# A layer of test-time training with a routed feed-forward block: GpSimd sums F for the bias, the inverse's join moves one place, and K and Q of 23 steps come from seven products of halves

## The chip, the core and the metric

The kernel runs on one NeuronCore of a Trainium2 chip. The core has a matrix engine (TensorE; PE in the profile, with its weight loads as PEld), a vector engine (VectorE, DVE), a scalar engine (ScalarE, ACT), a general one (GpSimd, POOL) and a queue that mostly issues transfers (SyncE, SP). Each engine works through its own instructions in order and waits for the others by semaphores. The metric is the time of one execution on the device in microseconds (us), the median of several runs.

## What is computed

The input is x, 2 sequences of 4096 tokens with 512 features. The first half of the block is a linear model that is trained while it reads: for every token, in order,

```python
pred = W @ k + b
g = 2.0 / d_h * (pred - v)
W = W - LR * jnp.outer(g, k)
b = b - LR * g
out = W @ q + b
```

with k, v, q = theta_K x, theta_V x, theta_Q x. Then x + out goes through a layer norm. The second half is a shared two-layer network plus the two best of eight experts for each token (a routed mixture), added to its input and normed again. Everything is float32.

## The kernel before

**Tiles and steps.** The tokens of both sequences are cut into 32 chunks of 128 (NCH = 32, and B = 2 sequences are handled side by side). Within a chunk the 128 sequential updates are solved at once: with A = 1 + K K^T of the chunk, the updates F are the solution of a triangular system, which the kernel gets by inverting a 128x128 triangular matrix. So the loop over chunks, not over tokens, is sequential: step c needs the W and b that step c-1 left.

**The parts of one round.** In round c four generators run beside each other, and their matmuls are woven together by `interleave`: it always advances the part whose yielded work is the smallest share of its total. The totals are numbers written out by hand.

- `step(c)`, total 49.0: R = -V + K W + b (`pr`, then the add L437 on VectorE with the bias tile `brep[s]`), the first part of the output (`po`, Q times W), the last part of the inverse (`join`), F (`pe`, copied by ScalarE to R, scaled by -BETA, L481), the output's correction with AQ (L485), the update of W (`pw` L491, added by VectorE L492), and the update of the bias: `pb` L497 multiplies F by a matrix of ones, which puts the sum of F over its 128 tokens in each of 128 partitions, and L498 adds that to `brep[s]`. GpSimd adds `brep[s]` to x ahead of the output (L439).
- `prep(c + 1)`, total 13.5: the next chunk's K and Q (`pkq` L327), their products `pa`, the block's diagonal parts sent through DRAM to L, and, for the chunks in `TURNED` (1 to 23), a copy of K transposed with the help of DRAM (`exchange`, later `turn_blocks` on VectorE). GpSimd masks A (L353) and copies the start value X (L361).
- `invert(c)`, total 95.0: the 32x32 diagonal blocks' inverses on VectorE (L372), then through DRAM to D and DT.
- `shared(c - 1)`, total 13.5: layer norm, the shared network and the router of the chunk before. GpSimd adds a bias (L627) and scatters the tokens' places with indirect transfers (L585).

From round 24 on the routed experts come in as a fifth part: `routed` gathers tokens (L809) and weights (L815) with indirect transfers on GpSimd's queue, each three tiles ahead. After that, `collect` fetches and sums the results.

**K and Q.** For each of theta_K and theta_Q, `prep` makes four blocks of 128 output features. Each block is 4 matmuls of 128x128 weights with the 256 tokens of both sequences as the moving operand; a float32 matmul stands in the profile as two MATMUL rows. So a chunk has 2 x 16 matmuls, 64 rows, of 256 columns. ScalarE copies the results to the tile KQ in 8 pieces (L334). The accumulators have the tag `pp`, of which there are two buffers, shared with `pa` and with the join's `pn` and `pz`.

**The join.** `join` is a generator of four pieces: one matmul pair with a copy by ScalarE (`pn`, N), then three times a matmul pair and an add by VectorE (`pz`, Z). `next(levels)` runs one. In the chunks 1 to 23 they come after the second sequence's R, in the middle and at the end of the first `po`, and in the middle of the second `po`; the last Z is Y, the left operand of `pe`.

**Orders.** On PE and VectorE instructions run in the order in which the program issues them (`manual_schedule`). For the other queues a scheduler sets the order, by when it reckons an instruction's inputs to be ready; each queue is then served strictly in that order.

Of the kernel before, what the change touches and what calls it, by code (L numbers as in the profile page):

```python
# [33 lines left out]

# [6 lines left out]
F32 = mybir.dt.float32  # L41
# [3 lines left out]
ALU = mybir.AluOpType  # L45
AX = mybir.AxisListType

P = 128
# [8 lines left out]
KQ_PACE, X_PACE, C_PACE = 1.0, 0.7, 10.0  # L57
PREP, INVERT = 13.5, 95.0
SKIP = 1 << 20

TURNED = range(1, 24)
PSUM = bass.MemoryType.PSUM
# [41 lines left out]
def postln_block(ctx: ExitStack, tc: tile.TileContext, x, xT, thK, thV, thQ, w0, b0, masks, blk,  # L104
# [211 lines left out]

    prepared, turned = {}, {}

    def prep(c):
        xt = xT_t[c]  # L320
        KQ = kqp.tile([P, DC, B, 2, P], F32, tag="kq", name=f"kq_{c}")
        for j, th in enumerate((thK_sb, thQ_sb)):
            for ec in range(0, DC, 2):
                ps = ps_p.tile([P, 2, B, P], F32, tag="pp", name=f"pkq_{c}_{j}_{ec}")
                for i in range(2):
                    for dc in range(DC):
                        nc.tensor.matmul(  # L327
                            ps[:, i].rearrange("p s t -> p (s t)"),
                            th[:, dc, (ec + i) * P:(ec + i + 1) * P],
                            xt[:, dc].rearrange("p s t -> p (s t)"),  # L330
                            start=(dc == 0), stop=(dc == DC - 1))
                    yield KQ_PACE
                for i in range(2):
                    nc.scalar.copy(KQ[:, ec + i, :, j, :], ps[:, i])  # L334
# [18 lines left out]
        nc.gpsimd.tensor_tensor(M, A1, mask[:, 0:1, :].broadcast_to([P, B, P]), ALU.mult)  # L353
# [7 lines left out]
        nc.gpsimd.tensor_copy(X, unit_sb)  # L361
# [55 lines left out]
    def step(c):  # L417
# [6 lines left out]
        for s in range(B):  # L424
            ps = ps_s.tile([P, D], F32, tag="ps", name=f"pr_{c}_{s}")
            for dc in range(DC):
                nc.tensor.matmul(ps, xt[:, dc, s, :], nthV_sb[:, dc, :],  # L427
                                 start=(dc == 0), stop=False)
                if dc % 2 == 1:
                    yield 2.0  # L430
            for ec in range(DC):
                nc.tensor.matmul(ps, KQ[:, ec, s, 0, :], W[s][:, ec, :],  # L432
                                 start=False, stop=(ec == DC - 1))
                if ec == 1:
                    yield 2.0
# [3 lines left out]
            nc.gpsimd.tensor_tensor(xc[:, s, :], xc[:, s, :], brep[s], ALU.add)  # L439
            if s == B - 1:  # L440
                next(levels)
            yield 2.5
        for s in range(B):

            ps = ps_s.tile([P, D], F32, tag="ps", name=f"po_{c}_{s}")
            for ec in range(DC):
                nc.tensor.matmul(ps, KQ[:, ec, s, 1, :], W[s][:, ec, :],  # L447
                                 start=(ec == 0), stop=False)
                if ec == 1:
                    if s == 0:  # L450
                        next(levels)
                    elif c in TURNED:
                        Y = next(levels)
                    yield 2.0
            O.append(ps)
            if s == 0:
                next(levels)
            yield 2.0
            if s == 0:

                if c not in TURNED:
                    Y = next(levels)
# [21 lines left out]
        for s in range(B):  # L484
# [3 lines left out]
            if c < NCH - 1:  # L488
                for ec in range(DC):
                    ps = ps_s.tile([P, D], F32, tag="ps", name=f"pw_{c}_{s}_{ec}")  # L490
                    nc.tensor.matmul(ps, K[s][:, ec, :], F[s], start=True, stop=True)  # L491
                    nc.vector.tensor_tensor(W[s][:, ec, :], ps, W[s][:, ec, :], ALU.add)  # L492
                    if s > 0 and ec == 1:
                        next(norm[0])
                    yield 1.0
                ps = ps_s.tile([P, D], F32, tag="ps", name=f"pb_{c}_{s}")
                nc.tensor.matmul(ps, ones, F[s], start=True, stop=True)  # L497
                nc.vector.tensor_tensor(brep[s], ps, brep[s], ALU.add)  # L498
# [222 lines left out]
    def plan(gr):  # L721
# [63 lines left out]
        sl = tmp("sl", [P, n])  # L785
# [275 lines left out]
```

## Time and profile before

| | |
|---|---|
| median of 3 runs | 2716.18 us (2708.08 to 2716.97) |
| the profiled execution | 2700.66 us, of which the span from first to last instruction is 2698.9 us |
| granted TensorE clock, mean | 0.986 |
| VectorE busy | 1272.1 us (47%), 4016 instructions |
| ScalarE busy | 759.8 us (28%), 1516 instructions |
| GpSimd busy | 763.3 us (28%), 767 instructions |
| K and Q matmuls (L327) | 2048 rows, busy 242.5 + 243.8 us |
| bias sums (`pb`, L497) | 124 rows, busy 63.8 us |
| bias adds (L498) | 62, mean 686 ns |

A group of the profile gives line, engine, operation, output and inputs by the program's names, the shapes, the number of instructions, their busy time and mean, and how long the engine was idle just before them and for what. Two cautions: a matmul's row lasts longer than the distance to the next one, since matmuls overlap in the array, so a PE that is "busy" need not be full; and the cost of a matmul in a stream is the distance between starts, not its row's length. A timeline's row merges equal neighbours: start, duration from the first start to the last end, and "x8" for eight of them.

The first step begins at 38.3 us and the steps 1 to 22 take 60.46 us each, from first `pr` to first `pr`. The rounds 24 to 27 with the routed tiles take 170, 166, 167 and 148 us, the rounds 28 to 30 between 67 and 75 us, and what follows the start of the last step 356 us.

### The profile page before, as it was taken

What the parts mean: (1) busy time and instruction counts of PE and PEld (TensorE: products, weight loads), DVE (VectorE), ACT (ScalarE), POOL (GpSimd) and SP (SyncE); (2) the same over time, 40 slices, a digit from 0 to 9 for tenths busy, and PEclk for the clock granted to TensorE, in tenths of its full rate; (3) what the DMA queues carried; (4) which work ended last, traced back from release to release, by engine and by line L of the source; (5) the groups of instructions that cost most, each with busy time, mean ns of one, the idle gap of its engine ahead of it and who ended that gap; (6) DMA issues with size and microseconds to landing.
All of it is one profiled execution on the core that took longest, in us unless ns stands there. A gap on an engine that the chain in (4) does not pass through costs nothing. (4 is left out here: it accounts for less than half of the span.)

```text
span 2698.9 us, 31214 instructions
## 1 busy us (share of the span) xinstructions
PE 2588.6 (96%) x10381; PEld 1654.4 (61%) x10381; DVE 1272.1 (47%) x4016; ACT 759.8 (28%) x1516; POOL 763.3 (28%) x767
## 2 busy tenths in 40 slices
PE   8999999999999999999999999999999989879887
PEld 5665666666656666666655666767666655446564
DVE  2555554455555554555556223232232466644245
ACT  1222222222222222222222232322223133434336
POOL 0111111111111111112123333343343334455555
PEclk9999999999999999999999999999999999989898
DMA  5122222222222222222233343353433345676677
GB/s 181 52 64 73 64 57 67 71 57 56 57 73 64 64 57 70 67 57 57 59 97 117 125 91 106 119 152 99 123 102 92 117 127 166 183 244 214 232 244 235
DMA packets 257712, 293.48 MB, mean 109 GB/s; under 512 B 158332, under 2 KB 171868, under 8 KB 253968
## 3 DMA queue, kind: packets, MB, share of 16 engines
q1 hardware_dynamic: 199536, 163.62, 20.1%
q0 software_dynamic: 49584, 111.61, 14.5%
q10 hardware_dynamic: 8432, 16.25, 1.9%
q8 instruction: 83, 1.36, 0.2%
q14 instruction: 77, 0.63, 0.1%
HBM read 345.43 MB, written 100.69 MB: 165 GB/s over the span
## 5 line engine op out<-in xcount | busy, mean ns | idle before, releaser
L372 DVE SCALAR_TENSOR_TENSOR X<-L,X 128x31 f32<-128x31 f32 (+22 forms) x1472 | 327.3, 269 | 26.3 <-DMA L<-dL 9.2
L833 PEld LDWEIGHTS phe<-gT,wb 128*128 128x128 f32 x2208 | 269.0, 193 | 63.7 <-issue 57.0
L847 DVE TENSOR_TENSOR o<-pye,wb 128x512 f32<-128x512 f32 x138 | 95.4, 691 | 427.3 <-PE pye L844 402.4
L844 PE MATMUL pye<-wb,he 128*128 128x512 f32 x552 | 273.4, 619 | 16.5 <-ACT he L837 15.5
L833 PE MATMUL phe<-gT,wb 128*128 128x128 f32 x2208 | 271.7, 277 | 8.1 <-DMA wb<-wcat_in,widx 6.8
L585 POOL DMA_INDIRECT gt<-code,ri x124 | 124.5, 1004 | 542.8 <-DVE ri L582 512.7
L491 PE MATMUL pw<-R,K 128*128 128x512 f32 x496 | 234.7, 604 | 15.7 <-DVE x L486 13.4
L327 PE MATMUL pkq<-xT,thK 128*128 128x256 f32 x1024 | 242.5, 381 | 7.4 <-DMA thK<-thK_in 7.4
L327 PE MATMUL pkq<-xT,thQ 128*128 128x256 f32 x1024 | 243.8, 382 | 2.7 <-DVE Z L411 2.7
L447 PE MATMUL po<-W,kq 128*128 128x512 f32 x512 | 245.9, 604 | 0.0
L815 POOL DMA_INDIRECT wb<-wcat_in,widx x138 | 145.3, 1053 | 332.1 <-DVE o L847 166.8
L327 PEld LDWEIGHTS pkq<-xT,thK 128*128 128x128 f32 x1024 | 195.1, 191 | 71.4 <-issue 49.0
L427 PE MATMUL pr<-thV,xT 128*128 128x512 f32 x512 | 238.0, 596 | 0.0
L432 PE MATMUL pr<-W,kq 128*128 128x512 f32 x512 | 231.9, 592 | 0.0
L837 ACT ACTIVATE he<-phe,wb 128x128 f32<-128x128 f32 x276 | 87.2, 364 | 422.0 <-PE phe L833 420.8
L327 PEld LDWEIGHTS pkq<-xT,thQ 128*128 128x128 f32 x1024 | 186.2, 191 | 28.2 <-issue 4.8
L492 DVE TENSOR_TENSOR W<-pw,W 128x512 f32<-128x512 f32 x248 | 168.3, 689 | 64.2 <-PE pw L491 63.7
L334 ACT COPY kq<-pkq 128x256 f32<-128x256 f32 x256 | 83.0, 375 | 407.7 <-PE pkq L327 407.7
L809 POOL DMA_INDIRECT g<-gy,gidx x138 | 139.3, 1009 | 134.2 <-PE pg L824 104.9
L844 PEld LDWEIGHTS pye<-wb,he 128*128 128x128 f32 x552 | 99.9, 192 | 119.8 <-issue 80.6
L491 PEld LDWEIGHTS pw<-R,K 128*128 128x128 f32 x496 | 89.7, 192 | 131.2 <-issue 76.3
L427 PEld LDWEIGHTS pr<-thV,xT 128*128 128x128 f32 x512 | 94.3, 190 | 99.5 <-issue 79.4
(207 smaller groups left out, 3366.6 us busy)
## 6 DMA issues: line engine op xcount, KB each, us to landing
ge<-o SPq DMA_DIRECT2D x138, 256.0 KB, 2.0
xT<-xT_in SPq DMA_DIRECT2D x32, 512.0 KB, 3.6
x<-x_in SPq DMA_DIRECT2D x32, 512.0 KB, 3.5
L<-dL SPq DMA_DIRECT2D x128, 128.0 KB, 2.9
gy<-x SPq DMA_DIRECT2D x31, 512.0 KB, 2.7
gb<-x SPq DMA_DIRECT2D x31, 512.0 KB, 2.7
acc<-gb POOLq DMA_DIRECT2D x31, 512.0 KB, 6.5
y_out<-acc ACTq DMA_DIRECT2D x31, 512.0 KB, 5.0
```

The lines of the kernel that those rows point to most:

```text
L327: nc.tensor.matmul(ps[:, i].rearrange("p s t -> p (s t)"), th[:, dc, (ec + i) * P:(ec + i + 1) * P], xt[:, dc].rearrange("p s t -> p (s t) ...
L372: nc.vector.scalar_tensor_tensor(X[:, h, j + 1:], L[:, j + 1:, j], X[:, h, j:j + 1], X[:, h, j + 1:], ALU.mult, ALU.add)
L427: nc.tensor.matmul(ps, xt[:, dc, s, :], nthV_sb[:, dc, :], start=(dc == 0), stop=False)
L432: nc.tensor.matmul(ps, KQ[:, ec, s, 0, :], W[s][:, ec, :], start=False, stop=(ec == DC - 1))
L447: nc.tensor.matmul(ps, KQ[:, ec, s, 1, :], W[s][:, ec, :], start=(ec == 0), stop=False)
L491: nc.tensor.matmul(ps, K[s][:, ec, :], F[s], start=True, stop=True)
L492: nc.vector.tensor_tensor(W[s][:, ec, :], ps, W[s][:, ec, :], ALU.add)
L585: nc.gpsimd.indirect_dma_start(out=gr.tables[s * K + k], out_offset=bass.IndirectOffsetOnAxis(ap=ri[:, s, k:k + 1], axis=0), in_=code[:, j ...
L809: nc.gpsimd.indirect_dma_start(out=g_t[k], out_offset=None, in_=gr.y, in_offset=bass.IndirectOffsetOnAxis(ap=gr.gidx[:, k:k + 1], axis=0), ...
L815: nc.gpsimd.indirect_dma_start(out=wbuf[k % NW], out_offset=None, in_=wcat, in_offset=bass.IndirectOffsetOnAxis(ap=gr.widx[:, k:k + 1], ax ...
L833: nc.tensor.matmul(ps[:, hc, :], w[:, dc * HF + hc * P:dc * HF + (hc + 1) * P], t[:, dc, :], start=(dc == 0), stop=(dc == DC - 1))
L844: nc.tensor.matmul(ps, h[:, hc, :], w[:, O2 + hc * D:O2 + (hc + 1) * D], start=(hc == 0), stop=(hc == HC - 1))
```

## The change

Three edits. First, the sum of F over the tokens is made on GpSimd (`partition_all_reduce` into a new tile `ar`, one buffer), and GpSimd adds it to the bias; the matmul with ones, its accumulator, the add on VectorE and the tile of ones go. Second, the four pieces of the join come one place later, and at the same places in all chunks: middle and end of the first `po`, middle and end of the second. Third, in the chunks 2 to 24 K and Q come from `seven`, Strassen's scheme: theta is split in halves of rows and columns, x in halves of the input features (low, high) and by sequence. The four blocks of a 2x2 by 2x2 product then take seven products of halves, of sums and differences of blocks, where the plain form takes eight. K and Q are done together (index j). The five combinations of theta are made once, at the start, in the buffers of the experts' weights, which are free until round 23; the five combinations of x are made in each round by GpSimd. Five of the seven products are copied out by ScalarE, GpSimd makes two sums of three of these, and VectorE adds each of the last four blocks from a product in PSUM and a saved tile.

The totals of `step` in `interleave` become 44.0 and 46.5. In `plan` the tile `sl` shares the buffer of `has`.

```diff
-    ones = const.tile([P, P], F32, tag="ones", name="ones")
-    nc.gpsimd.memset(ones, 1.0)
...
+    comb = [[] for _ in range(5)]
+    for i, th in enumerate((thK_sb, thQ_sb)):
+        a11, a21, a12, a22 = (th[:, d:d + DC // 2, e:e + D // 2] for d in (0, DC // 2)
+                              for e in (0, D // 2))
+        t = wbuf[i][:, 0:5 * D].rearrange("p (n d e) -> p n d e", n=5, d=DC // 2)
+        for n, (p, q, op) in enumerate(((a11, a22, ALU.add), (a21, a22, ALU.add),
+                                        (a11, a12, ALU.add), (a21, a11, ALU.subtract),
+                                        (a12, a22, ALU.subtract))):
+            nc.gpsimd.tensor_tensor(t[:, n], p, q, op)
+            comb[n].append(t[:, n])
...
+    def seven(c, KQ):
...
+        for n, (p, q, op) in enumerate(((b11, b22, ALU.add), (b12, b22, ALU.subtract),
+                                        (b21, b11, ALU.subtract), (b11, b12, ALU.add),
+                                        (b21, b22, ALU.add))):
+            nc.gpsimd.tensor_tensor(sums[:, n], p, q, op)
+        saved, made = {}, {}
+
+        def product(name, half, x_half):
+            ps = ps_p.tile([P, DC // 2, 2, P], F32, tag="pp", name=f"pkq_{c}_{name}")
+            made[name] = ps
+            for i in range(DC // 2):
+                for j in range(2):
+                    for dc in range(DC // 2):
+                        nc.tensor.matmul(ps[:, i, j, :], half[j][:, dc, i * P:(i + 1) * P],
+                                         x_half[:, dc, :],
+                                         start=(dc == 0), stop=(dc == DC // 2 - 1))
+
+        def save(name, tag):
+            m = cp.tile([P, DC // 2, 2, P], F32, tag=tag, name=f"m{name}_{c}")
+            nc.scalar.copy(m, made[name])
+            saved[name] = m
+
+        def block(h, s, name, other):
+            nc.vector.tensor_tensor(KQ[:, h, s], made[name], saved[other], ALU.add)
...
+        def total(name, tag, p, q, r, op):
+
+            d = cp.tile([P, DC // 2, 2, P], F32, tag=tag, name=f"m{name}_{c}")
+            nc.gpsimd.tensor_tensor(d, saved[p], saved[q], op)
+            nc.gpsimd.tensor_tensor(d, d, saved[r], ALU.add)
+            saved[name] = d
+
+        pace = 8 * KQ_PACE / 7
+        product(5, comb[2], b22)
+        save(5, "z00")
+        yield pace
+        product(4, half_of(high, 1), sums[:, 2])
+        save(4, "z01")
+        yield pace
+        product(1, comb[0], sums[:, 0])
+        save(1, "z10")
+        total("451", "z01", 4, 5, 1, ALU.subtract)
+        yield pace
+        product(2, comb[1], b11)
+        save(2, "z11")
+        block(high, 0, 2, 4)
+        yield pace
+        product(3, half_of(low, 0), sums[:, 1])
+        save(3, "z00")
+        block(low, 1, 3, 5)
+        total("123", "z10", 1, 2, 3, ALU.subtract)
+        yield pace
+        product(7, comb[4], sums[:, 4])
+        block(low, 0, 7, "451")
+        yield pace
+        product(6, comb[3], sums[:, 3])
+        yield pace
+        block(high, 1, 6, "123")
+        yield 0.3
...
             nc.gpsimd.tensor_tensor(xc[:, s, :], xc[:, s, :], brep[s], ALU.add)
-            if s == B - 1:
-                next(levels)
             yield 2.5
...
                 if ec == 1:
-                    if s == 0:
-                        next(levels)
-                    elif c in TURNED:
-                        Y = next(levels)
+                    next(levels)
                     yield 2.0
             O.append(ps)
-            if s == 0:
-                next(levels)
+            Y = next(levels)
             yield 2.0
...
-                ps = ps_s.tile([P, D], F32, tag="ps", name=f"pb_{c}_{s}")
-                nc.tensor.matmul(ps, ones, F[s], start=True, stop=True)
-                nc.vector.tensor_tensor(brep[s], ps, brep[s], ALU.add)
-                yield 1.0
+
+                ar = stepp.tile([P, D], F32, tag="ar", name=f"ar_{c}_{s}", bufs=1)
+                nc.gpsimd.partition_all_reduce(ar, F[s], P, bass_isa.ReduceOp.add)
+                nc.gpsimd.tensor_tensor(brep[s], ar, brep[s], ALU.add)
...
-        parts = [(49.0, step(c))]
+        parts = [(44.0 if c in TURNED else 46.5, step(c))]
```

More of the change, by code (lines that the diff above doesn't have):

```diff
@@ L35 @@
 import concourse.bass as bass
+import concourse.bass_isa as bass_isa
 import concourse.tile as tile
@@ L59 @@
 SKIP = 1 << 20
+SEVEN = range(2, 25)
 TURNED = range(1, 24)
@@ L317, in postln_block, with half_of @@
     prepared, turned = {}, {}
+    def seven(c, KQ):
+        xt = xT_t[c]
+        low, high = slice(0, DC // 2), slice(DC // 2, DC)
+        b11, b12, b21, b22 = (xt[:, h, s, :] for h in (low, high) for s in range(B))
+        sums = wbuf[2][:, (c % 2) * 5 * D // 2:(c % 2 + 1) * 5 * D // 2].rearrange(
+            "p (n d t) -> p n d t", d=DC // 2, t=P)
+        for n, (p, q, op) in enumerate(((b11, b22, ALU.add), (b12, b22, ALU.subtract),
[18 more added lines that the diff above has]
+            nc.vector.tensor_tensor(KQ[:, h, s], made[name], saved[other], ALU.add)
+        def half_of(h, k):
+            return [t[:, h, k * D // 2:(k + 1) * D // 2] for t in (thK_sb, thQ_sb)]
+        def total(name, tag, p, q, r, op):
[30 more added lines that the diff above has]
+        yield 0.3
@@ L321, in prep @@
         KQ = kqp.tile([P, DC, B, 2, P], F32, tag="kq", name=f"kq_{c}")
[L322 to L334, printed above, removed]
+        if c in SEVEN:
+            yield from seven(c, KQ)
+        else:
+            for j, th in enumerate((thK_sb, thQ_sb)):
+                for ec in range(0, DC, 2):
+                    ps = ps_p.tile([P, 2, B, P], F32, tag="pp", name=f"pkq_{c}_{j}_{ec}")
+                    for i in range(2):
+                        for dc in range(DC):
+                            nc.tensor.matmul(
+                                ps[:, i].rearrange("p s t -> p (s t)"),
+                                th[:, dc, (ec + i) * P:(ec + i + 1) * P],
+                                xt[:, dc].rearrange("p s t -> p (s t)"),
+                                start=(dc == 0), stop=(dc == DC - 1))
+                        yield KQ_PACE
+                    for i in range(2):
+                        nc.scalar.copy(KQ[:, ec + i, :, j, :], ps[:, i])
         A1 = prepp.tile([P, B, P], F32, tag="A1", name=f"A1_{c}", bufs=1)
@@ L449, in step @@
                 if ec == 1:
-                    if s == 0:
-                        next(levels)
-                    elif c in TURNED:
-                        Y = next(levels)
+                    next(levels)
                     yield 2.0
             O.append(ps)
-            if s == 0:
-                next(levels)
+            Y = next(levels)
             yield 2.0
             if s == 0:
-                if c not in TURNED:
-                    Y = next(levels)
                 if c < NCH - 1:
@@ L784, in plan @@
         nc.vector.tensor_tensor(adj, adj, step[:, None, :].broadcast_to(full), ALU.mult)
-        sl = tmp("sl", [P, n])
+        sl = tmp("has", [P, n], "sl")
         nc.vector.tensor_reduce(sl, adj, AX.X, ALU.add)
```

## The prediction

> **What bounds the kernel now.** I read the page's busy shares and slices first, then one steady round in a table of stretches, then the timelines of PE and of GpSimd inside it. The page:
>
> ```profile
> span 2698.9 us, 31214 instructions
> ...
> PE 2588.6 (96%) x10381; PEld 1654.4 (61%) x10381; DVE 1272.1 (47%) x4016; ACT 759.8 (28%) x1516; POOL 763.3 (28%) x767
> ...
> PE   8999999999999999999999999999999989879887
> ...
> POOL 0111111111111111112123333343343334455555
> ```
>
> PE is at 9 from the second slice to the 32nd; GpSimd at 1 up to the 18th. "Busy" can mislead on PE, so I take distances between starts. PE's timeline of round 24 has all three widths side by side:
>
> ```profile
> 1511.71 1.88 PE L844 MATMUL pye<-wb,he 128*128 128x512 f32 x4
> 1513.42 1.89 PE L327 MATMUL pkq<-xT,thK 128*128 128x256 f32 x8
> 1515.15 1.95 PE L833 MATMUL phe<-gT,wb 128*128 128x128 f32 x16
> 1516.93 0.60 PE L824 MATMUL pg<-ident,g 128*128 128x128 f32 x4
> ```
>
> Start to start: 4 rows of 512 columns in 1.71 us (0.427 each), 8 of 256 in 1.73 (0.215), 16 of 128 in 1.78 (0.111). Columns are all that is paid for. With 0.427, 0.213 and 0.107 us a row, one round of steps 1 to 22 adds up to: `pkq` 64 x 0.213 = 13.65, `pr` 32 x 0.427 = 13.65, `po` and `pw` 6.83 each, `pa`, `ph` and `py` 3.4 to 3.5 each, `pe`, AQ, `pb` and the join 1.71 each, transposes and router 1.6: 59.7 us. The round lasts 60.46. So PE is full to 0.75 us, and what leaves PE leaves the time, as long as nothing else becomes late.
>
> **Removed from PE.** `pb` is 4 rows of 512 a round: 4 x 0.427 = 1.71 us, in 31 rounds 52.9 us. Two adds on VectorE (L498, 0.69 us) go with it. K and Q: seven products of 8 matmuls, 56 matmuls, 112 rows of 128 columns: 112 x 0.107 = 11.95 us against 13.65, so 1.71 us a round and 39.3 us in 23 rounds. Together **92.2 us** at most, 3.42 us of a round of 60.46.
>
> Here a rule speaks against the change. The Trainium skill, "TensorE: Matmul & The Clock Gate", section "Back-to-back issue gap", gives for streams of weight load and matmul about 81 ns at 128 columns and 131 ns at 512: a column costs 2.5 times more in narrow matmuls. Halfway between (some 106 ns at 256, my estimate), a narrow column would cost 1.5 times that of `pkq`: 112 rows would take 18.3 us, and the 23 rounds would lose 107 us. The row of `phe`, with new weights for each of its 16 rows, shows 0.111 against 0.215; even that 0.111 leaves 112 x 0.111 = 12.4. The trace decides: 12.0 to 12.4 us.
>
> **Other engines.** ScalarE: 8 copies of 0.375 us (L334) become 5 of 128x512, by the row of L606 0.61: 3.0 us both times. VectorE: four new adds from PSUM at 0.69 (the row of L492), two fewer: +1.4 us on 36.8 a round of 57; it stays under the cover of PE. If an add is late, the next product waits, as `pp` has two buffers; I put 0.3 us a round on this. The once-made combinations of theta are 10 GpSimd adds of 1.27 us (the row of L439), 12.7 us at the start, where GpSimd stands idle to 23.09 us; they are needed after 87 us: nothing. No transfer is added. That of K through DRAM (`exchange`) now waits for the last block instead of the middle of the round, some 18 us later on SP's queue; its reader is the next round's `turn_blocks` over 40 us on, and its landing took 2.7 and 3.0 us: nothing. In round 23 the first weight gathers wait for the last products that read those buffers; a few us of GpSimd, covered.
>
> **The join one place later.** I weave the parts by hand with the new totals. Behind the last `pz` PE has one `py` (1.7 us) before `pe`, and Z takes 0.28 + 0.42 plus signals: covered. Between first and second `pz` stands half a `po` (1.7 us): covered. In step 0 `pn` waited 3.76 us for D; half a `po` now goes first: about 1 us gained, not counted. The removed last place before the second half of `po` costs nothing.
>
> **GpSimd is what is new on the path.** Its steady round now:
>
> ```profile
> 1035.33 1.03 POOL L585 DMA_INDIRECT gt<-code,ri  x1 [23.60 <-DVE ri L582]
> ...
> 1039.23 0.98 POOL L585 DMA_INDIRECT gt<-code,ri  x1 [0.30 <-issue]
> 1046.33 0.72 POOL L353 TENSOR_TENSOR A<-A,mask 128x256 f32<-128x256 f32 x1 [6.12 <-DMA dL<-A]
> 1050.06 1.27 POOL L439 TENSOR_TENSOR x<-x,brep 128x512 f32<-128x512 f32 x1 [3.01 <-DVE brep L498]
> 1055.43 1.26 POOL L439 TENSOR_TENSOR x<-x,brep 128x512 f32<-128x512 f32 x1 [4.11 <-DVE brep L498]
> 1062.10 2.49 POOL L627 TENSOR_TENSOR x<-x,b 128x512 f32<-128x512 f32 x2 [5.41 <-PE pt L604]
> 1072.06 0.24 POOL L361 COPY X<-unit 128x64 f32<-128x64 f32 x1 [7.46 <-DMA dX<-X]
> ```
>
> Ten us of work in 60. Added: 5 sums of 128x256 at 0.73 (L353) = 3.6; 4 adds of 128x512 at 1.27 for the two totals = 5.1; 2 bias adds = 2.5; and two all-reduces of length *a* each. The sum with gaps between scatters is 22 + 2a. A second unknown is *r*, the price of a change between all-reduce and ordinary add, of which each round has four.
>
> Bounds. *a*: no row shows it. From below, one pass of 128x512 on this engine is 1.27 us, and it must be read and written while 128 partitions are summed: two passes, 2.5 us. From above, the Trainium skill, "GPSIMD Engine Reference", section "Cross-partition — where GPSIMD wins", has 247.7 us for a reduction over partitions at 128x2048, which makes 62 us at 512 columns (estimate). The ends are far apart; nearest is the row of 1.27 us, and I take 5 to 6 passes, **7 us** (an estimate from that row). *r*: GpSimd's rows of different kinds follow each other with no gap (a gather of 1.00 us at 1517.81, the copy X at 1518.81), so 0 from below; the same page, section "Instruction dispatch", has about 6 us for the first call after a kernel's code has been loaded. I take the rows' value, near **0**, and keep 6.
>
> The deadline. In the woven order F of the first sequence is ready at about 42 us of a round of 57, behind it the scatters end near 46. R of the second sequence (L437), which needs the second bias, comes at 25 us of the next round, and VectorE is strictly in order: behind R stands the add that frees the accumulator which the sixth product in line needs, so PE stalls from about 27. That leaves 38 us, less 8 for what else is in line (bias adds 2.5, A 0.7, the two of L439 2.5, L627 2.5): PE feels nothing while **2a + 3r < 30**, and GpSimd has room while 2a + 4r < 35. My values give 14. If r is 6, they give 32 and 38, just over.
>
> In rounds 24 to 27 token gathers stand behind the all-reduces. They are issued three tiles, some 17 us, ahead, and land in 8.5: a block of 8 us is nearly covered, and 8 such blocks cost about 8 us. The fetches of rounds 28 to 30 (6 blocks) lose about 6.
>
> **Sum.** 92.2 - 7 (0.3 us in 23 rounds) - 8 - 6 = 71 us, 2.6%. The profiled execution would go from 2700.66 to 2630 us; the median lies 15.5 above that execution and goes to **2645 us**. With nothing lost it is 2624; with double the losses 2666.
>
> **Rivals.**
> - GpSimd late (slower): each round waits for the bias. It decides above 2a + 3r = 30, and turns the sign at about 34, when the overrun eats 3.4 us a round; r = 6 with a = 9 is 36, or 42 of GpSimd's own time against 35: a round of about 64, +3.5 us in 23 rounds = +80, and in the routed rounds 14 blocks of 22 us, each some 5 past its cover, +70, less 12 for `pb`: about 2850. For it speaks the page's 6 us; against it GpSimd's idle 50 us and gapless rows. Chance 0.33.
> - All-reduce at the price of the page's reduction, 62 us: a GpSimd round of 146 us, +86 in 31 rounds: about 5400. Against it: GpSimd's adds here are within 2 to 4 times a VectorE add, far from 50 times; 0.04.
> - Narrow matmuls as the rule has them: +107 - 53 + 21 = +75, about 2790. Against it stands the row of `phe`; 0.02.
> - Gain and overrun cancel (2a + 3r near 33): 2708 to 2724; 0.05.
> - The products don't shorten K and Q because PE waits for sums or accumulators, but `pb`'s gain stays: 2716 - 53 + 14 = 2677. Against: each product has about 5 us till the buffer is needed again. 0.08, faster.
>
> The likeliest, 0.48, is 2645 with a range of 2620 to 2670. A measurement can tell about 0.3% (8 us) from no change. Faster 0.56, same 0.05, slower 0.39. The range runs from 2612 to 2850: it holds the forecast, the smaller gain, the tie and most of the late cases.
>
> **What would show it.** Right: rounds of 57.0 to 57.5 us from `pr` to `pr`, 112 `pkq` rows of 128x128 at 0.107 apart, R of both sequences waiting for PE, not for GpSimd, and all-reduces under 10 us. Wrong: L437 waiting for GpSimd's bias with PE idle behind it, gaps after each all-reduce on GpSimd, or `pg` waiting for its gather.

## The result, and where the time went

The changed kernel takes **2872.05 us** in the median (2846.91 to 2884.71, 4 runs) beside 2716.57 us before (4 runs): 1.057 times the time, 95% interval 1.049 to 1.064. The forecast of 2645 us was wrong in sign, and the time lies above the range. The profiled execution took 2884.71 us. Its page, with the all-reduce's group (busy time and mean in ns, then the idle time before it):

```profile
span 2882.0 us, 33659 instructions
...
PE 2596.1 (90%) x11361; PEld 1705.1 (59%) x11361; DVE 1476.3 (51%) x4046; ACT 765.3 (27%) x1444; POOL 1254.8 (44%) x1107
...
PE   8999899899999899998998899999999998768887
...
POOL 2434434434443443444343534444343435555545
...
L575 POOL PARTITION_ALL_REDUCE ar<-R x62 | 201.4, 3249 | 436.0 <-issue 397.5
```

PE's row has 8s where it had 9s. GpSimd stands at 3 and 4 from the second slice on, and ahead of 62 all-reduces of 3.25 us lie 436 us of idle time, in 397.5 of which it waited for nothing that the profile shows ("issue"). By stages (cut at the first `pr` of a step, us of each trace; the profiled execution after is the slowest of its four and that of before, 2700.66 us, is faster than its other runs, so that the differences add up to 183 us where the medians are 155 apart):

| stage | before | after | difference |
|---|---|---|---|
| start and step 0 | 86.9 | 81.9 | -5.0 |
| steps 1 to 22 | 1330.1 | 1440.8 | +110.7 |
| step 23 | 63.0 | 83.2 | +20.3 |
| rounds 24 to 27 | 650.8 | 675.3 | +24.5 |
| rounds 28 to 30 | 212.1 | 230.2 | +18.1 |
| from step 31 on | 356.1 | 370.5 | +14.4 |

The steps 1 to 22 decide. Step 1 still takes 58.17 us; the steps 2 to 22 take 64.2 to 68.4, mean 65.84. Their rows at the forecast's prices make 56.30 us. Of the other 9.5, PE has no row running in 5.6 us, always waiting for a result of VectorE (`chosen` 2.8, Z 2.2, a block of K and Q 0.5). It loses another 2.5 us because it works 5.1 us at a granted clock of 0.50, half of the full one. Most of the rest is there without any waiting too (57.53 us in `e7` below, PE idle 0.01). A round before and the round shown below, with busy times and the granted clock (PEclk):

```profile
core 0: us, PE busy (x) PEld busy (x) DVE busy (x) ACT busy (x) POOL busy (x), PEclk, DMA share, GB/s
993.80:1054.20 60.40, 60.40 (x214) 37.07 (x213) 32.42 (x109) 14.31 (x27) 9.99 (x10) 1.00 0.24 62
1062.20:1127.20 65.00, 59.71 (x259) 38.70 (x258) 40.47 (x111) 14.63 (x24) 26.11 (x23) 0.95 0.31 69
```

GpSimd ahead of that round and in it (start, duration, what it waited for in brackets):

```profile
1051.06 0.97 POOL L662 DMA_INDIRECT gt<-code,ri  x1 [0.30 <-issue]
1058.70 3.25 POOL L575 PARTITION_ALL_REDUCE ar<-R  x1 [6.67 <-issue]
1069.83 1.26 POOL L576 TENSOR_TENSOR brep<-ar,brep 128x512 f32<-128x512 f32 x1 [7.88 <-ACT yT L683]
1071.05 0.72 POOL L438 TENSOR_TENSOR A<-A,mask 128x256 f32<-128x256 f32 x1
1077.59 3.25 POOL L575 PARTITION_ALL_REDUCE ar<-R  x1 [5.82 <-issue]
1087.73 1.26 POOL L524 TENSOR_TENSOR x<-x,brep 128x512 f32<-128x512 f32 x1 [6.89 <-issue]
1088.96 1.25 POOL L576 TENSOR_TENSOR brep<-ar,brep 128x512 f32<-128x512 f32 x1
```

Here each change between an all-reduce and another kind of instruction is preceded by 5.8 to 7.9 us of nothing (called a load below), and there are four of them, because `ar` has one buffer: the second all-reduce can't start until the first sum has been added, by an instruction of the other kind. The trace has two MODIFY_POOL_CONFIG at each, 250 in all; before it has 2. A gather behind an all-reduce has no such pause: from round 24 on 11 of them start 0.20 us behind one, and 7.0 to 8.6 us of idle time come ahead of the next ordinary instruction. From the last scatter to the second bias 38.2 us go by. All the adds that GpSimd has besides (x, the totals of three saved products, the sums of x) come behind that, at 25 to 40 us of the round. VectorE's router in a round before, then VectorE at that place after, and PE:

```profile
1023.81 0.16 DVE L622 TENSOR_TENSOR lg<-pre,eb 128x16 f32<-128x16 f32 x1
1024.01 0.18 DVE L515 SCALAR_TENSOR_TENSOR u<-lg 128x16 f32<-128x16 f32 x1
...
1027.70 0.16 DVE L519 TENSOR_SCALAR w<-u 128x16 f32<-128x16 f32 x1
1027.77 0.28 DVE L528 TENSOR_TENSOR gt<-lg 128x128 f32<-128x128 f32 x1
```

```profile
1090.25 0.69 DVE L522 TENSOR_TENSOR R<-pr,brep 128x512 f32<-128x512 f32 x1 [3.75 <-POOL brep L576]
1090.86 0.68 DVE L361 TENSOR_TENSOR kq<-pkq,m 128x512 f32<-128x512 f32 x1
1091.45 1.26 DVE L699 TENSOR_TENSOR lg<-pre,eb 128x16 f32<-128x16 f32 x1
1092.75 1.19 DVE L592 SCALAR_TENSOR_TENSOR u<-lg 128x16 f32<-128x16 f32 x1
1094.22 0.94 DVE L596 TENSOR_SCALAR w<-u 128x16 f32<-128x16 f32 x1 [0.28 <-ACT u L593]
1095.07 1.43 DVE L605 TENSOR_TENSOR gt<-lg 128x128 f32<-128x128 f32 x1
...
1103.47 0.17 DVE L633 TENSOR_SCALAR chosen<-rank 128x16 bf16<-128x16 f32 x1
```

```profile
1091.86 1.95 PE L351 MATMUL pkq<-wb,wb 128*128 128x128 f32 x16
...
1095.81 1.88 PE L530 MATMUL po<-W,kq 128*128 128x512 f32 x4
1100.05 0.71 PE L494 MATMUL pz<-Z,N 128*128 128x128 f32 x4 [2.36 <-DVE Z L496]
1103.69 0.20 PE L642 MATMUL pq<-chosen,before 128*128 128x8 bf16 x2 [2.93 <-DVE chosen L633]
...
1103.83 3.76 PE L351 MATMUL pkq<-wb,wb 128*128 128x128 f32 x16
```

Three things are to be seen. VectorE idles 3.75 us ahead of R, until the bias comes; the products that R also needs ended 2.6 us before it. The router's small operations behind it, 0.16 to 0.28 us each before, take 0.9 to 1.4 us while GpSimd's adds run. And PE waits 2.36 us for a Z and 2.93 for the router's `chosen`, after which 16 rows of 128 columns take 3.76 us where 16 others take 1.95: the granted clock is 0.50 from 1101.0 to 1107.9 us and 1.00 before and after. (The Trainium skill, "TensorE: Matmul & The Clock Gate", Part 1, has half clock after about 3.4 us of little work, and the full clock back after as long at work; here it drops 3.3 us after the first of these waits begins and is back 4.2 us after PE works again, which agrees.) The two waits, 5.3 us, cost 7.

### The profile page after: what moved, and what is told of

It reads as the page before. It is cut to its first block, busy times and chain, and to the rows that moved or that the text cites. A ratio compares the mean times of both kernels' runs of the same rounds, so it can differ in the third digit from the quotient of the medians.

```text
span 2882.0 us, 33659 instructions
## 1 busy us (share of the span) xinstructions
PE 2596.1 (90%) x11361; PEld 1705.1 (59%) x11361; DVE 1476.3 (51%) x4046; ACT 765.3 (27%) x1444; POOL 1254.8 (44%) x1107
## 4 chain that ended last, share of the span: by engine, by line
PE 52%; issue 16%; DVE 13%; POOL 9%; DMA 5%; ACT 3%; POOLq 0%; SPq 0%; DVEq 0%; ACTq 0%
PE pw L568 7%; PE pye L921 7%; PE phe L910 6%; PE pkq L351 5%; PE pr L512 4%; PE py L735 3%; PE pkq L412 3%; PE po L530 3%; PE pa L425 3%; POOL ar L575 3%; POOL brep L576 2%; PE pr L517 2%; PE po L562 2%; PE pg L901 2%; DMA wb<-wcat_in,widx 2%
## 5 line engine op out<-in xcount | busy, mean ns | idle before, releaser
L575 POOL PARTITION_ALL_REDUCE ar<-R x62 | 201.4, 3249 | 436.0 <-issue 397.5
L457 DVE SCALAR_TENSOR_TENSOR X<-L,X 128x31 f32<-128x31 f32 (+22 forms) x1472 | 336.8, 278 | 28.9 <-DMA L<-dL 11.9
L921 PE MATMUL pye<-wb,he 128*128 128x512 f32 x552 | 277.9, 627 | 18.1 <-ACT he L914 15.9
L910 PE MATMUL phe<-gT,wb 128*128 128x128 f32 x2208 | 278.0, 281 | 15.9 <-DMA wb<-wcat_in,widx 14.3
L530 PE MATMUL po<-W,kq 128*128 128x512 f32 x512 | 259.9, 632 | 0.0
L568 PE MATMUL pw<-R,K 128*128 128x512 f32 x496 | 240.7, 608 | 12.4 <-DVE x L563 11.5
L351 PE MATMUL pkq<-wb,wb 128*128 128x128 f32 x1104 | 174.8, 325 | 11.0 <-DVE kq L361 11.0
L351 PEld LDWEIGHTS pkq<-wb,wb 128*128 128x128 f32 x1104 | 165.9, 236 | 24.6 <-DVE kq L361 13.6
L576 POOL TENSOR_TENSOR brep<-ar,brep 128x512 f32<-128x512 f32 x62 | 78.1, 1260 | 196.8 <-issue 95.1
L524 POOL TENSOR_TENSOR x<-x,brep 128x512 f32<-128x512 f32 x64 | 80.7, 1262 | 190.1 <-issue 173.7
L962 POOL DMA_INDIRECT z<-ge,sidx x124 | 130.8, 1055 | 63.4 <-issue 26.5
```

The source lines that it names most:

```text
L351: nc.tensor.matmul(ps[:, i, j, :], half[j][:, dc, i * P:(i + 1) * P], x_half[:, dc, :], start=(dc == 0), stop=(dc == DC // 2 - 1))
L457: nc.vector.scalar_tensor_tensor(X[:, h, j + 1:], L[:, j + 1:, j], X[:, h, j:j + 1], X[:, h, j + 1:], ALU.mult, ALU.add)
L530: nc.tensor.matmul(ps, KQ[:, ec, s, 1, :], W[s][:, ec, :], start=(ec == 0), stop=False)
L575: nc.gpsimd.partition_all_reduce(ar, F[s], P, bass_isa.ReduceOp.add)
L910: nc.tensor.matmul(ps[:, hc, :], w[:, dc * HF + hc * P:dc * HF + (hc + 1) * P], t[:, dc, :], start=(dc == 0), stop=(dc == DC - 1))
L921: nc.tensor.matmul(ps, h[:, hc, :], w[:, O2 + hc * D:O2 + (hc + 1) * D], start=(hc == 0), stop=(hc == HC - 1))
```

## The experiments

"Ratio" is to the kernel before, run beside it, with the 95% interval; "steps" are the mean of steps 2 to 22 in the one profiled execution of each kernel. In the diffs "+" is the kernel tried, and unless another is named, it starts from the kernel after.

### The parts, one at a time

**Bias sums back on PE**, the rest of the change kept (`e1`; the totals of `step` 46.0 and 48.5):

```diff
-                nc.gpsimd.partition_all_reduce(ar, F[s], P, bass_isa.ReduceOp.add)
-                nc.gpsimd.tensor_tensor(brep[s], ar, brep[s], ALU.add)
+                nc.tensor.matmul(ps, ones, F[s], start=True, stop=True)
+                nc.vector.tensor_tensor(brep[s], ps, brep[s], ALU.add)
```

> The change with the bias sum back on PE and VectorE (pb and its add), so GpSimd never changes between two kinds of instruction; the seven products and the moved join stay. Theory A (the code loads around each all-reduce make the bias late, and all else follows from that): steps 1 to 22 fall from about 65.5 us to 58.0 of matmul columns plus about 0.8 of waits, VectorE's router instructions are short again, the median is about 2680. Rival B (GpSimd's new adds slow VectorE down, whatever the all-reduce does): the slow router instructions and the waits for Z and for the router stay, rounds of 62 us and more, median over 2760.

Ratio 1.0014 (0.9995 to 1.0033). The loss goes with the all-reduce. But little is gained: the steps are 59.66 us, 0.80 less than before where the columns are 1.71 less, and step 23 with 76.1 us gives most of these 18 us back.

**The all-reduce alone**, in the kernel before (`e2`; the diff above the other way round, old K and Q, old join).

> The kernel before with the all-reduce alone: no seven products, join where it was. Theory A: the gaps of about 7 us stand around each all-reduce here too, the second bias is ready late in the next round, R waits for GpSimd, and with the join right behind R the rounds of 58.0 us of columns take 61 to 65 us; median 2740 to 2850. Rival B (the added sums and totals are needed for the loss): R hardly waits, rounds of 58.7, median about 2680.

Ratio 1.0045 (1.0028 to 1.0061). The steps are 58.68 us: the full gain of 1.78, with the same four loads a round. So the loads alone don't hurt the steps, nor do the products alone; they do together. The gain of 39 us is lost from round 24 on (+66 us), where the loads stand among the gathers on GpSimd's queue.

**The same up to step 23**, PE's sums after it (`e10`, from `e2`; edit: `if c < 24` around the all-reduce, whose result goes to a buffer of tag z11).

> The kernel before with the all-reduce alone, and only in the steps up to 23; from step 24 on PE sums F as before. In the run with all-reduces in every step the steps 1 to 22 took 58.67 us and the whole was no shorter than before. Theory L (what was lost there came from the late rounds alone, where the code loads stand between the gathers on GpSimd): the steps stay at 58.6 to 58.8, round 23 at 65, the rounds 24 to 30 and the end go back to those of the kernel before, and the time is 2716 less 22 times 1.79 = 39 us, plus 0 to 5: about 2680 us, a ratio of 0.985 to 0.989. Rival: the plan or the transfers of the late rounds are set back by something that stays (the first gathers late, or another order of the queues): the late rounds stay longer than before by 30 us or more, ratio 0.997 or above.

Ratio 0.9914 (0.9898 to 0.9931), between the two. Of the 66 us, 40 came back: rounds 25 to 30 are within 4 us of those before. Round 24 (184.6 us, before 170.0) and the end (366.9, before 356.1) stay long; why wasn't found.

**The join at its old places** (`e4`):

```diff
+            if s == B - 1:
+                next(levels)
...
-                    next(levels)
+                    if s == 0:
+                        next(levels)
+                    elif c in TURNED:
+                        Y = next(levels)
```

> The change with the join's places as they were before. Theory A: the join is no cause; with the first pz sooner behind the late R, PE waits about as long or up to 3 us a round longer, median 2870 to 2940. Rival C (the later join is what leaves Z and pe without cover): rounds fall below 62 us, median under 2790.

Ratio 1.0300 (1.0281 to 1.0319), 2791.67 us, and steps of 61.66 us: far from theory A, and what rival C had, save that the time is 1.7 us over its limit of 2790. When VectorE is late, the later join costs 4.2 us a step, since a Z then stands in VectorE's order behind what is late. The start is longer by 4.7 us.

### The number of loads

**Two loads a round** (`e3`): up to step 23 both all-reduces stand side by side, each with its own buffer, and VectorE adds the bias just ahead of R; from step 24 on PE sums F.

```diff
+                if c < 24:
+                    ar = cp.tile([P, D], F32, tag="z11", name=f"ar_{c}_{s}")
+                    nc.gpsimd.partition_all_reduce(ar, F[s], P, bass_isa.ReduceOp.add)
+                    summed[s] = ar
...
+            if s in summed:
+                nc.vector.tensor_tensor(brep[s], summed.pop(s), brep[s], ALU.add)
```

> The change with the two all-reduces of a step next to each other and the adds to the bias on VectorE just ahead of R, so two code loads a round instead of four; from step 24 on the bias sum is back on PE. Theory A: 22 us of adds and scatters + 6.5 + 14 us of loads fit in the round, both biases are there before R, rounds of 57.0 to 58 us, median about 2640. Rival B: the adds for sums and totals stay as many, so rounds stay over 61 us, median over 2740.

Ratio 0.9816 (0.9797 to 0.9835), steps 57.76 us. Two things were changed at once up to step 23, so a second run left the adds on GpSimd (`e14`, from `e3`):

```diff
                     summed[s] = ar
+                    if s == 1:
+                        for t in range(B):
+                            nc.gpsimd.tensor_tensor(brep[t], summed[t], brep[t], ALU.add)
```

> The run with two loads (all-reduces next to each other up to step 23, PE's sums after it), with the bias adds back on GpSimd behind the second all-reduce, as in the kernel after. If the number of loads is the cause, the bias still comes in time: F of the second sequence at about 42 us of a round, all-reduce 3 us and load 7 us, so about 53, some 20 us before its R; the steps 1 to 22 take 57.5 to 59 us and the ratio is 0.978 to 0.990. If the gain of that run came from taking the adds to VectorE, the steps are 62 us or more and the ratio is above 1.00.

Ratio 0.9844 (0.9827 to 0.9861), steps 57.70 us: 8.1 us less than in the kernel after, by the order of one queue and a second buffer. GpSimd in a round of it:

```profile
1002.44 6.49 POOL L577 PARTITION_ALL_REDUCE ar<-R  x2 [8.36 <-issue]
1015.63 1.27 POOL L581 TENSOR_TENSOR brep<-ar,brep 128x512 f32<-128x512 f32 x1 [6.71 <-issue]
1016.87 0.73 POOL L440 TENSOR_TENSOR A<-A,mask 128x256 f32<-128x256 f32 x1
1017.55 1.26 POOL L581 TENSOR_TENSOR brep<-ar,brep 128x512 f32<-128x512 f32 x1
```

**The full line without late bias** (`e5`, from `e1`: PE makes the bias, and GpSimd's line is filled up to step 23).

```diff
+                    nc.gpsimd.partition_all_reduce(ar, F[s], P, bass_isa.ReduceOp.add)
+                    nc.gpsimd.tensor_tensor(ar, ar, ar, ALU.add)
```

> The bias sum on PE as in e1, but the all-reduces still run up to step 23, each with an add behind it that nobody reads: four code loads a round and the same line on GpSimd as in the change, only without the bias depending on it. Theory A1 (what costs is R, late by the bias): rounds as in e1, 59.65 us, to 60.5. Theory A2 (the loads fill GpSimd's line, and the totals, the sums and VectorE next to the bunched adds are late, whatever R does): rounds of 62 us and more.

Ratio 1.0418 (1.0391 to 1.0444), steps 64.63 us, though no R waits for GpSimd. That the late bias is the whole cause falls here. With the same work in another order, both all-reduces first and then both adds (`e13`):

> The run with idle all-reduces (bias from PE, totals on GpSimd), changed in the order of GpSimd's queue alone: up to step 23 the two all-reduces stand next to each other and the two unread adds behind both, so two changes of kind a round and not four. Same work, some 14 us less of loading. If the loads are what fills GpSimd's line and makes the steps 64.6 us long, they fall to 59.6 to 60.5 us, as without any all-reduce, and the ratio from 1.042 to 1.000 to 1.008. If it is the all-reduces and adds themselves (their time, or VectorE slowed beside them), the steps stay above 62 us and the ratio above 1.02.

Ratio 1.0121 (1.0103 to 1.0139), steps 60.33 us. Halving the loads at equal work takes away 4.3 of the 5.0 us. The ratio is above what was expected, since step 23 (82.2 us) and the rounds 24 to 27 (676) stay long.

### How it reaches PE

**Totals on VectorE** in the kernel after (`e8`):

```diff
-            nc.gpsimd.tensor_tensor(d, saved[p], saved[q], op)
-            nc.gpsimd.tensor_tensor(d, d, saved[r], ALU.add)
+            nc.vector.tensor_tensor(d, saved[p], saved[q], op)
+            nc.vector.tensor_tensor(d, d, saved[r], ALU.add)
```

> The change with the four adds for the two totals on VectorE instead of GpSimd: the second bias is ready as late as before (it stands ahead of most of these adds in the line), but GpSimd's bunch of adds behind it is 5 us shorter. If the lateness of R is all, rounds stay at 64 to 66 us. If VectorE's slow instructions next to the bunch are half of the loss, rounds fall to about 61 to 63.

Ratio 1.0595 (1.0568 to 1.0622). Most of the router's operations were short again (`lg` 0.20 us) and nothing was gained. I read this as proof that slow VectorE operations are not the cause. That was wrong, as a control shows below, and as the trace shows too: the first two of the adds moved to VectorE now stand where `lg` stood, beside GpSimd's adds, and take 1.77 and 1.64 us (0.68 and 0.69 for the other two). The delay had only passed to other VectorE operations. The same edit on `e5`, so that neither bias nor totals come from GpSimd (`e9`):

> The kernel after with the bias summed on PE, the totals of three saved products added on VectorE, and up to step 23 the two all-reduces, each with an unread add behind it, left on GpSimd, so that its line is as full as in the kernel after. Theory A2 (GpSimd's line is full, and exactly two of its results are waited for: the bias by R, the totals by the last blocks of K and Q): with both taken off that line nothing that PE needs comes from it, the steps 2 to 22 fall from the 64.6 us of the run with idle all-reduces to 59.5 to 60.5, as without any all-reduce, and the time goes to 2705 to 2725 us, a ratio of 0.995 to 1.005. Rival: the full line hurts in a third way (the sums of x for the products, the mask of A and the inverse behind it, the x that is added into y, or the slower VectorE beside it): the steps stay at 62 us or more and the ratio at 1.02 or more.

Ratio 1.0387 (1.0366 to 1.0409), steps 64.37 us: A2 falls. The control is that kernel without its all-reduces (`e11`):

> The kernel after with the bias summed on PE and no all-reduce, and the totals of three saved products added on VectorE: the run before this one without its all-reduces. It is the control for it. Theory C (GpSimd's line, pushed back by the code loads, runs its adds of x and its sums beside VectorE's totals and router and makes them longer, and that is the third way): without the loads these adds run earlier, VectorE's four adds of 0.69 us fit in its idle time, the steps 2 to 22 take 59.5 to 60.5 us and the ratio is 0.998 to 1.006. Rival: four more adds on VectorE ahead of Z and the router are late by themselves: steps of 62 us or more, ratio 1.02 or more, and then the run before says nothing of GpSimd.

Ratio 1.0160 (1.0140 to 1.0179), steps 61.41 us, between the two. The edit costs 1.75 us a step by itself: four adds ahead of the router, and an order on ScalarE in which h of the shared network goes ahead of the router's u, so that w waits 3.2 us (0.3 in `e1`). So `e8` does not clear VectorE, and in `e9` 3.0 us a step still come from GpSimd's full line. With the join's old places (`e12`, from `e9`):

> The run with idle all-reduces and the totals on VectorE, with the join's four pieces put back to their old places. Theory J (the later join took the slack: each Z now stands on VectorE just behind R or the router, and PE asks for it 1 to 2 us after; with the old places the same lateness meets slack): the steps 2 to 22 fall from 64.3 us to 58.5 to 60 and the ratio from 1.039 to 0.995 to 1.01. Rival: the lateness reaches PE by pq and the products whatever the place of Z: steps of 62 us or more, ratio 1.025 or more.

Ratio 1.0304 (1.0287 to 1.0322), steps 63.19 us: theory J misses, 1.2 us of these 3.0 are the join's.

What is left is VectorE itself. **Eight unread adds on GpSimd beside the router** (`e15`, from `e11`; no load, nothing late):

```diff
             R.append(r)
+            if s == 1 and c < 24:
+                t = cp.tile([P, D], F32, tag="z11", name=f"t_{c}")
+                for _ in range(8):
+                    nc.gpsimd.tensor_tensor(t, r, r, ALU.add)
```

> The run with PE's bias sums, no all-reduce and the totals on VectorE, to which eight unread GpSimd adds of 128x512 a step are added (up to step 23), reading the second sequence's R, so that they run at 27 to 37 us of a round, beside VectorE's router. No change of kind, and nothing that PE needs comes from GpSimd late. Theory P (GpSimd's adds, which the loads have pushed to that place, hold up VectorE's operations that read two tiles from SBUF; from R to the router's choice VectorE is busy 13.4 us in the kernel after, 6.7 before): VectorE's busy time there rises from 7.4 to 11 us or more, and the steps 2 to 22 go from 61.4 to 64 to 67 us, ratio 1.03 to 1.06. Rival Q (the longer operations fill waits that are there anyway; the loss comes from late results alone): the steps stay at 61.4 to 62 us, ratio 1.015 to 1.02.

Ratio 1.0440 (1.0399 to 1.0480), steps 64.86 us. VectorE with these adds, and the same three instructions in `e11`:

```profile
1020.77 1.41 DVE L372 TENSOR_TENSOR m<-m,m 128x512 f32<-128x512 f32 x1
1022.11 1.00 DVE L705 TENSOR_TENSOR lg<-pre,eb 128x16 f32<-128x16 f32 x1
...
1026.54 1.06 DVE L602 TENSOR_SCALAR w<-u 128x16 f32<-128x16 f32 x1 [3.22 <-ACT u L599]
```

```profile
974.71 0.69 DVE L372 TENSOR_TENSOR m<-m,m 128x512 f32<-128x512 f32 x1
975.32 0.17 DVE L701 TENSOR_TENSOR lg<-pre,eb 128x16 f32<-128x16 f32 x1
...
978.92 0.17 DVE L598 TENSOR_SCALAR w<-u 128x16 f32<-128x16 f32 x1 [3.22 <-ACT u L595]
```

Three instructions are 0.7 to 0.9 us longer each (in 14 of the steps 2 to 22 the third is `gt`, 0.28 to 1.13 us, in the other 7 it is `w`), `chosen` comes 2.0 us later, PE waits for Z and `pq` and then runs at half clock (0.50 in 3.2 us of its work), and the step is 3.45 us longer. **The same adds at another place** (`e16`: reading F of the second sequence, at 49 to 58 us of the round):

> The same eight unread adds, reading the second sequence's F instead, so that they run from 47 to 57 us of a round, where VectorE adds products from PSUM to W and y. By theory P these operations read one operand from PSUM and the place has slack: VectorE's busy time from R to the choice stays at 7.4 us and the steps at 61.4 to 62 us, ratio 1.015 to 1.02. If eight more adds on GpSimd cost by their mere number, the steps are as long as in the run with the adds beside the router.

Ratio 1.0185 (1.0144 to 1.0225), steps 61.48 us: no effect. Theory P holds. Of the operations with one input in PSUM, W's add takes 0.69 us in all 68 cases in which GpSimd's adds cover it. Means, us from the step's first `pr`, over steps 3 to 21, in the last three columns over steps 2 to 22. "VectorE busy" adds up the durations; "lost to clock" is half of the time that PE works at a granted clock of 0.50:

| kernel | second R done | VectorE busy, R to `chosen` | `pq` starts | PE idle | lost to clock | steps |
|---|---|---|---|---|---|---|
| before | 26.1 | 6.7 | 39.4 | 0.0 | 0.0 | 60.46 |
| all-reduce alone | 28.2 | 8.5 | 39.4 | 0.0 | 0.0 | 58.68 |
| PE sums (`e1`) | 26.3 | 6.7 | 36.4 | 0.4 | 0.0 | 59.66 |
| idle all-reduces (`e5`) | 26.5 | 12.5 | 39.9 | 3.7 | 1.5 | 64.63 |
| idle, two loads (`e13`) | 29.4 | 8.4 | 37.1 | 1.0 | 0.0 | 60.33 |
| two loads (`e14`) | 28.4 | 8.1 | 36.2 | 0.2 | 0.0 | 57.70 |
| after | 29.3 | 13.4 | 42.0 | 5.6 | 2.5 | 65.84 |

The late R is not the cause by itself: R of `e14` is nearly as late as that of the kernel after. VectorE's busy time is what differs. And the start of `pq` says why the all-reduce alone is harmless: with the old K and Q, PE asks for the router at 39.4 us and `chosen` is there 2.2 us earlier; with seven products it already stands idle 0.4 us for it at 36.4. Idle time and clock make up the whole of a step's excess: without them the kernel after takes 57.8 us and `e14` 57.5, and the three with PE's sums 59.3 to 59.4.

### A version that beats both

`SEVEN` one chunk shorter, so that step 23 has the old K and Q (`e6`, from `e3`; `range(2, 24)`), and with the join's old places besides (`e7`):

> e3 with the seven products only up to chunk 23, so that no block of K and Q waits on VectorE behind the plan of the first group in round 23. If that queue is what made round 23 some 17 us longer, round 23 falls from 79.8 us to about 65 and the median by about 13 us, from 0.982 of the kernel before to about 0.977. If it was the weight buffers that prep(24) read (a write after a read), likewise; if it was something else, round 23 stays near 80.

> e6 with the join's places as they were before. With both biases in time, theory A has no use for the later join: rounds within 0.5 us of e6's 57.5, the median within 0.5%. If the later join is bad by itself (its adds meet the bunch of GpSimd's adds, and Z stands nearer to pe), rounds fall to about 57.0; if it is good by itself, they rise over 58.

Ratios 0.9806 (0.9785 to 0.9828) and 0.9803 (0.9782 to 0.9824), both 2656.27 us. Step 23 falls from 79.8 to 70.5 and 63.8 us; what the old join gains there it loses at the start (87.0 us against 82.0). With the biases in time the join's place is worth nothing either way.

## Why the prediction was wrong

**What held.** What leaves PE leaves the step, once nothing else is late: `e2` gains 1.78 us a step of 1.71 forecast for `pb`, and `e14` 2.76 of the 3.42 for both. 16 narrow rows take 1.79 us from start to start (1091.86 to 1093.65), 0.112 each, not what the rule for narrow matmuls would have had; 112 of them are 12.5 us, at the upper end of the forecast's 12.0 to 12.4. The all-reduce itself takes 3.25 us, half of the estimated 7 and near the two passes of the lower bound. Rival 1 (GpSimd late, step of about 64, 2850 us) came nearest: 65.84 and 2872. That is in part luck: its reason was that each round waits for the bias, and `e5` loses 5.0 us a step against `e1` where none does.

**Two steps failed.** The first is the price of a change of kind: "I take the rows' value, near **0**". The rows quoted for it, a gather and then a copy, are not of the kind in question, so they bounded nothing. The upper end was right: 5.8 to 7.9 us, beside the 6 us of the Trainium skill ("GPSIMD Engine Reference", "Instruction dispatch"), and ahead of every all-reduce and of the next ordinary instruction behind it, not only at a first call.

**The limits were wrong too.** With the measured a = 3.25 and the four gaps above (27.3 us, 6.8 each), 2a + 3r is 27 and 2a + 4r 34: both within the limits of 30 and 35, and no loss would have been forecast. Ahead of the second bias stand four changes, not three: the first can't begin until the scatters have ended. 6.5 + 27.3 + 4.5 us of adds is 38.3 us of the 38 that there were.

**The second is a cost put at nothing without a reason.** VectorE was charged its own added instructions, 1.4 us a round, and "GpSimd has room" was asked of time alone, not of what runs beside it. The Trainium skill, "SBUF — State Buffer", "SBUF: two separate sides", says that a VectorE operation with two inputs in SBUF and a GpSimd operation that reads SBUF exclude each other for a whole instruction. That speaks against this change, and I didn't weigh it. The traces agree: `lg` grows from 0.16 by up to the 1.1 us that an add of 1.27 can hold it, while R (one input in PSUM, 0.69) and the reduction L610 (0.29) keep their length. `w`, with one input, was held as well (0.94 us in every one of these steps), so the rule for two inputs does not cover all of it. VectorE was 6.7 us longer busy from R to `chosen`; with that and a second R 3.3 us later than before, PE lost 5.6 us a step in idle time and 2.5 to the clock. Without the loads the loss is gone (`e1`), and adds beside the router bring 3.45 us of it back without any load (`e15`).

**Smaller steps.** "Rounds 24 to 27 lose 8, 28 to 30 lose 6": 24.5 and 18.1, and 14.4 more at the end. Round 23, "covered": +20.3 us. There the last block of K and Q stands on VectorE behind the whole plan of the routed part, and PE waits 8.17 us for it ahead of the second `pa`, and earlier in the step 7.8 us for `chosen` (the granted clock of the step is 0.90):

```profile
1579.65 0.16 DVE L808 TENSOR_TENSOR count<-next,first 128x8 f32<-128x8 f32 x1
...
1590.93 0.68 DVE L361 TENSOR_TENSOR kq<-pkq,m 128x512 f32<-128x512 f32 x1
```

```profile
1591.67 3.78 PE L425 MATMUL pa<-kq 128*128 128x256 f32 x8 [8.17 <-DVE kq L361]
```

"0.3 us a round" for VectorE's lateness with the products: `e1` gains 0.9 less than the columns say, of which 0.4 is the wait for `chosen` and most of the rest the price of 0.112 for 0.107 a row. "The join one place later: covered": true only when VectorE is in time; the start gained 5 us instead of 1. GpSimd's adds "within 2 to 4 times a VectorE add": 1.27 to 0.69 us, 1.8 times.

**Open**: the long round 24 and end of `e10`. Of the 8.1 us between the kernel after and `e14`, 5.4 are idle time of PE and 2.5 clock. Behind them stand a late second R and a held-up VectorE, and the table has each nearly alone: R in time and VectorE busy for 12.5 us costs 5.0 us a step (`e5` against `e1`), R as late as in the kernel after and VectorE busy for 8.4 costs 0.7 (`e13` against `e1`). How much more the two make together is not separated. `e15` shows that the held-up VectorE suffices, not that it is all. A kernel after with no adds beside the router wasn't tried.

## To carry to other kernels

Before work goes to an idle engine, count how often its queue changes between kinds of instruction, and look for a row that shows just that change: two buffers and one order took four loads to two, and a step from 65.84 to 57.70 us. Ask also where in the round the moved work will run and which engine reads the same memory at that time; a full gain in one half of a change can hang on slack that the other half takes away. And an experiment that moves a cost needs a control that moves it with nothing else to relieve.

## What the hardware showed that was not expected

- Summing 128x512 float32 over 128 partitions on GpSimd takes 3.25 us, only 2.6 times an ordinary add of that size (1.27); the change to it, and from it to an ordinary instruction, costs 5.8 to 7.9 us each in the round shown. A gather started 0.20 us behind it.
- Beside GpSimd's adds, VectorE operations of 0.16 to 0.28 us took up to 1.2 to 1.4 us; those with one input in PSUM kept their 0.69.
- Two waits of PE, 2.36 and 2.93 us with 0.7 us of work between, left the granted clock at 0.50 for 6.8 us: the next 16 rows of 128 columns took 3.76 us for 1.95.
